# A graph network on one core: sums of messages turned so that their columns lie on partitions

## The chip, the cores and the metric

The kernel runs on one core of a Trainium2 chip. The metric is device time in microseconds (us). Before the change three runs took 4106.76, 4111.01 and 4119.22 us, so the median is 4111.01 us. Lower is better.

The engines are named as in the profile: PE multiplies matrices and PEld is its loading of the side that stays in the array; DVE and ACT work elementwise; POOL here issues the indirect transfers (gathers and scatters); SP issues the plain ones. A product names two operands: the *loaded* side (written into the array first, up to 128 columns) and the *moving* side (streamed through it, up to 512 columns). The result has the loaded side's columns on partitions and the moving side's columns along the free axis. Results go to PSUM.

## The reference

The input is a graph of 6250 nodes with 128 features each and 106250 edges, sorted by destination. Each edge has 64 features and one of 4 types. The first layer is an attention over edges by type, with residual. The second layer, which the change concerns, is:

```
h    = relu(layernorm(x))
e    = concat(h[src_full], h[dst_full], ef_full)      # edges in both directions
msg  = leaky_relu(e @ We1) @ We2                      # 320 -> 256 -> 128
red  = segment_sum(msg, dst_full)                     # per node
x    = x + leaky_relu(concat(h, red) @ Wn1) @ Wn2     # 256 -> 256 -> 128
```

Here `src_full = concat(src, dst)` and `dst_full = concat(dst, src)`, so that each edge sends one message to its destination and one to its source. Since `We2` is linear, the kernel sums the 256 hidden columns per node first and multiplies the sums by `We2` once per node.

## The kernel before

All data are float32. Nodes are packed in 50 blocks (`NU`) of 126: two halves of 63 nodes, each on 64 partitions. Edges of a block are laid in two lots (q = 0, 1) of 9 x 128 places, so that one *step* handles two tiles of 128 edges, and a block takes 9 steps (`TB`); 450 steps in all. After the first layer a table `abtab` holds, per node, both halves of its hidden contribution (2 x 256 columns), and `h2t` holds the transposed node features.

**The loop over edges (lines 1085 to 1137).** For each step: POOL gathers rows of `abtab` by source, two transfers, seven steps ahead (`gather_pair`, issued at line 85). PE forms `z` from edge features and the destination's rows (line 1105). DVE adds the gathered rows (1107), ACT multiplies by 0.01 (1108), DVE takes the maximum (1109): `s` now holds, per edge, 256 columns of the message to the destination and 256 of the message to the source. ACT appends the source's number (1110). POOL scatters the second half to a table `m2d` in memory, two transfers (1113). `s` has four buffers, and a buffer is free again when its scatter has landed and its sums are done.

The message to the destination is summed at once: at lines 1124 to 1126 PE multiplies a one-hot matrix `oh` (128 edges x 64 nodes of a half, the loaded side) with `s` (128 edges x 256 columns, the moving side), into 64 partitions of the PSUM tile `sums`, accumulating over the block's nine steps. Then `add_sums` (979) copies (ACT, 984) or adds (DVE, 982) `sums` into `racc`, an SBUF tile with nodes on partitions and 256 columns for each block.

**The windows (987 to 1018).** The scattered messages, ordered by source in `m2d`, are read back by plain transfers: five parts (`NPT`) of 50 windows, one window per block. A window has 3 to 5 tiles of 128 rows (`window_tiles`): a base of 4, or 3 in the last part, and one more for the blocks near the part's own edges. There are 1012 tiles in all. For each tile DVE makes a one-hot matrix `ohw` (1015), and PE multiplies it (loaded) with the 256 columns of the tile (moving) into `sums2` (1016); the window's sums are added to `racc`. Part j begins in the loop at block `DONE[j]` = 11, 22, 32, 43 and its windows are spread over the steps up to the next one; 11, 10, 11 and 7 blocks. The fifth part follows the loop.

**The last stage (1140 to 1147).** The fifth part's windows run with `node_update` (903) after every four blocks. It transposes `racc` on PE, block by block and half by half (908 to 913: eight transposes and two ACT copies for four blocks), multiplies by `w2` (916), copies to `rdT`, multiplies `hT` and `rdT` by `wn1t` (922, 924), applies the leaky maximum (926), multiplies by `wn2t` (930), adds the residual (938) and writes out (939).

**What sets the order.** The program is written step by step, and a scheduler of the language orders the instructions on each engine by its own estimates of cost; each engine then runs its list strictly in turn. A float32 product is two instructions on PE in this trace: 900 products at line 1105 are 1800 rows.

Of the kernel before, what the change touches and what calls it, by code (L numbers as in the profile page):

```python
# [9 lines left out]
F32 = mybir.dt.float32  # L10
# [4 lines left out]
ALU = mybir.AluOpType  # L15
# [6 lines left out]
P = 128  # L22
# [7 lines left out]
HID = 256  # L30
# [14 lines left out]
NU = -(-N // DB)  # L45
NBK = 2 * NU
NROW = NU * DB + 4
TB = 9
# [41 lines left out]
def kernel(ctx: ExitStack, tc: tile.TileContext, x, src, dst, ef, et, w_rel, a_src, a_dst,  # L90
# [10 lines left out]
    nc = tc.nc  # L101
    ts_, tt, stt, red = (nc.vector.tensor_scalar, nc.vector.tensor_tensor,
                         nc.vector.scalar_tensor_tensor, nc.vector.tensor_reduce)
# [17 lines left out]
    ident = const.tile([P, P], F32, name="ident")  # L121
# [76 lines left out]
    with ExitStack() as prep:  # L198
        cpool = prep.enter_context(tc.tile_pool(name="prep", bufs=1))
        wpool = prep.enter_context(tc.tile_pool(name="prep2", bufs=2))  # L200
        pp = prep.enter_context(tc.tile_pool(name="prepp", bufs=2, space=PSUM))
# [148 lines left out]
        w = CG * TB  # L350
# [541 lines left out]


    c3 = fast.enter_context(tc.tile_pool(name="c3", bufs=1))
    racc = c3.tile([P, NU, HID], F32, name="racc")
    w2 = c3.tile([P, 2, C], F32, name="w2")
    nc.scalar.dma_start(w2, we2.rearrange("(a k) f -> k a f", k=P))
    wn1t = c3.tile([P, 2, HID], F32, name="wn1t")
# [4 lines left out]
    def node_update(wp, pp, b0, nbs):  # L903

        w = nbs * P
        hT = wp.tile([P, 4 * P], F32, name="hT")
        nc.sync.dma_start(hT[:, 0:w], h2t[:, b0 * P:b0 * P + w])
        rT = wp.tile([P, 2, 4 * P], F32, name="rT")
        for a in range(2):
            tp = pp.tile([P, 4 * P], F32, name="tp")  # L910
            for i in range(nbs):
                nc.tensor.transpose(tp[:, i * P:(i + 1) * P], racc[:, b0 + i, a * P:(a + 1) * P], ident)
            nc.scalar.copy(rT[:, a, 0:w], tp[:, 0:w])
        ps = pp.tile([P, 4 * P], F32, name="tp")
        for a in range(2):
            nc.tensor.matmul(ps[:, 0:w], w2[:, a, :], rT[:, a, 0:w], start=(a == 0), stop=(a == 1))
        rdT = wp.tile([P, 4 * P], F32, name="rdT")
        nc.vector.tensor_copy(rdT[:, 0:w], ps[:, 0:w])
        hid = wp.tile([P, 2, 4 * P], F32, name="hid")
        for a in range(2):  # L920
            ph = pp.tile([P, 4 * P], F32, name="ph")
            nc.tensor.matmul(ph[:, 0:w], wn1t[:, 0, a * P:(a + 1) * P], hT[:, 0:w],
                             start=True, stop=False)
            nc.tensor.matmul(ph[:, 0:w], wn1t[:, 1, a * P:(a + 1) * P], rdT[:, 0:w], start=False, stop=True)
            nc.scalar.copy(hid[:, a, 0:w], ph[:, 0:w])
        stt(hid[:, :, 0:w], hid[:, :, 0:w], 0.01, hid[:, :, 0:w], op0=ALU.mult, op1=ALU.max)
        for i in range(nbs):
            po = pp.tile([P, C], F32, name="ph")
            for a in range(2):
                nc.tensor.matmul(po, hid[:, a, i * P:(i + 1) * P], wn2t[:, a, :], start=(a == 0), stop=(a == 1))  # L930
            xr = wp.tile([P, C], F32, name="xr")
            y = wp.tile([P, C], F32, name="y")
            n0 = (b0 + i) * DB
            for q in range(2):
                n1, n2 = n0 + q * GB, min(n0 + q * GB + GB, N)
                h = slice(q * 64, q * 64 + n2 - n1)
                nc.sync.dma_start(xr[h, :], x1r[n1:n2, :])
                tt(y[h, :], po[h, :], xr[h, :], op=ALU.add)  # L938
                nc.sync.dma_start(out[n1:n2, :], y[h, :])
# [5 lines left out]
    with ExitStack() as s4:  # L945
# [33 lines left out]
        def add_sums(b, sums):  # L979

            if b in begun:
                tt(racc[:, b, :], racc[:, b, :], sums, op=ALU.add)
            else:
                nc.scalar.copy(racc[:, b, :], sums)
                begun.add(b)

        def windows(j):

            mts = {}

            def load(b):
                n = window_tiles(j, b)
                mt = mp.tile([P, 5, MW], F32, name="mt")
                r = first_of(st1, j * NU + b, 1, PLACES - n * P)[0]
                ld = nc.sync.dma_start(mt[:, 0:n, :], m2d[ds(r, n * P), :].rearrange("(p i) c -> p i c", i=n))
                if j < NPT - 1:
                    tc.declare_no_dep(ld.ins, group=f"late{j}",
                                      reason="blocks behind a part's last one have no edge of it, or all is done again")
                tc.add_to_no_dep_group("m2", ld.ins)
                mts[b] = mt  # L1000

            for b in range(2):
                load(b)
            yield
            for b in range(NU):
                if b + 2 < NU:
                    load(b + 2)
                n = window_tiles(j, b)
                mt = mts.pop(b)
                at = mp.tile([P, 5], F32, name="at")  # L1010
                ts_(at[:, 0:n], mt[:, 0:n, HID], float(-b * DB), None, op0=ALU.add)
                sums = ps2.tile([P, HID], F32, name="sums2")
                for i in range(n):
                    oh = mp.tile([P, P], F32, name="ohw", bufs=4)
                    ts_(oh, col, at[:, i:i + 1], None, op0=ALU.is_equal)  # L1015
                    nc.tensor.matmul(sums, oh, mt[:, i, 0:HID], start=(i == 0), stop=(i == n - 1))  # L1016
                add_sums(b, sums)
                yield

        with ExitStack() as s5:  # L1020
# [64 lines left out]
            for u in range(NU):  # L1085
                lt, oh = blk.pop(u)
                c0 = 2 * u * TB
                nxt_ = ready(u + 1) if u + 1 < NU else iter(())
                more = u % 5 == 2 and 2 * u + 6 < NBK
                plcs = places(wp, bank, (2 * u + 6) // CG) if more else iter(())  # L1090
                if u in DONE[:-1]:
                    for _ in wins:
                        pass
                    j = DONE.index(u)
                    wins = windows(j)
                    slots = (DONE[j + 1] - u) * TB - 4
                    taken = 0
                sums = pt.tile([P, HID], F32, name="sums")
                for i in range(TB):
                    n = u * TB + i  # L1100
                    if n + AHEAD < NU * TB:
                        gather_pair(n + AHEAD)
                    z = pz.tile([P, 2, 2 * HID], F32, name="z")
                    for q in range(2):
                        nc.tensor.matmul(z[:, q, :], lt[q][:, i * P:(i + 1) * P], rhs[(2 * u + q) % 4], start=True, stop=True)  # L1105
                    s = wp.tile([P, 2, 2 * HID + 1], F32, name="s", bufs=4)
                    tt(s[:, :, 0:2 * HID], z, ags.pop(n), op=ALU.add)  # L1107
                    nc.scalar.mul(z, s[:, :, 0:2 * HID], 0.01)  # L1108
                    tt(s[:, :, 0:2 * HID], s[:, :, 0:2 * HID], z, op=ALU.max)  # L1109
                    nc.scalar.copy(s[:, :, 2 * HID], srcf[:, c0:c0 + 2 * TB].rearrange("p (q i) -> p q i", q=2)[:, :, i])  # L1110
                    for q in range(2):
                        k = c0 + q * TB + i
                        st = nc.gpsimd.indirect_dma_start(  # L1113
                            out=m2d, out_offset=bass.IndirectOffsetOnAxis(ap=placei[:, k:k + 1], axis=0),
                            in_=s[:, q, HID:HID + MW], in_offset=None)
                        tc.declare_no_dep(st.ins, group="m2", reason="each place is written once, and read behind its part")
                        tc.add_to_no_dep_group("m2", st.ins)
                        for j in range(NPT - 1):
                            if u >= DONE[j]:
                                tc.add_to_no_dep_group(f"late{j}", st.ins)  # L1120
                    next(nxt_, None)
                    if i in (1, TB - 1):
                        next(plcs, None)
                    for q in range(2):
                        nc.tensor.matmul(sums[q * 64:(q + 1) * 64, :], oh[:, q * TB + i, :], s[:, q, 0:HID],  # L1125
                                         start=(i == 0), stop=(i == TB - 1))
                    if u >= DONE[0]:

                        t = (u - DONE[sum(u >= d for d in DONE) - 1]) * TB + i
                        while taken * slots <= (t - 2) * (NU + 1):  # L1130
                            next(wins, None)
                            taken += 1
                for _ in nxt_:
                    pass
                add_sums(u, sums)
# [587 lines left out]
```

## Time and profile before

| | before |
|---|---|
| median of three runs | 4111.01 us |
| profiled execution: time, and span within it | 4104.87 us, 4103.1 us |
| mean granted PE clock | 0.878 |
| PE busy | 3053.0 us, 74% of the span |
| POOL busy | 2892.2 us, 70% |
| DVE busy | 2738.6 us, 67% |
| ACT busy | 1545.1 us, 38% |
| edge sums, line 1125, PE | 335.2 us, 1800 instructions |
| window sums, line 1016, PE | 523.3 us, 2024 instructions |
| transposes of `racc`, line 912, PE | 17.6 us, 100 instructions |
| copies of the transposes, line 913, ACT | 13.5 us, 26 instructions |

How to read it: a row of a group gives the line, the engine, the operation, output and inputs, the shapes, how many, and then the busy time in us and the mean duration of one in ns. Durations of PE instructions include the way through the array, so that neighbours overlap; the distance from start to start tells what one costs in a row. A row of the timeline merges neighbours of one kind (`x4`): the start, the time from the first's start to the last's end, and in brackets the idle time of the engine ahead of it with what ended it. "issue" is time in which the engine waited for nothing that the profile shows. The clock that PE was granted stands in the tables by stage (1.00 is full).

### The profile page before, as it was taken

The numbers are of one execution on the slowest core, as the hardware profiler recorded it, in microseconds if no ns is written. First come the engines' busy times: TensorE is split into PE (matmuls) and PEld (weight loads), VectorE is DVE, ScalarE is ACT, GpSimd is POOL, SyncE is SP. The second block draws the span as 40 slices with busy tenths as digits, with TensorE's granted clock in tenths as the row PEclk, the third lists the DMA queues.
The fourth block names the chain that finished last, engine by engine and source line by source line (L and its number), as shares of the span: only waits on it lengthen the run. The fifth ranks groups of instructions, "written<-read, shape, count | busy, mean of one in ns | idle before, by whom it ended". The sixth has DMA issues, their size and how long they took to land. (4 is left out here: it accounts for less than half of the span.)

```text
span 4103.1 us, 43438 instructions
## 1 busy us (share of the span) xinstructions
PE 3053.0 (74%) x11258; PEld 1729.4 (42%) x11258; DVE 2738.6 (67%) x5139; ACT 1545.1 (38%) x2990; POOL 2892.2 (70%) x2887
## 2 busy tenths in 40 slices
PE   4468877778887756666678877778768777688888
PEld 3346555555555532222234342334324333244455
DVE  7467888887777745555466665666657666577755
ACT  3256655566666622222223333222222322222211
POOL 5777787777777527777777777777777777777600
PEclk9669978899999978888899898999989998899999
DMA  7544444455555356666587886888868878588754
GB/s 193 160 101 122 115 114 115 116 123 121 122 129 127 92 135 186 178 178 182 164 252 236 254 249 183 246 245 242 248 198 259 246 234 248 174 260 272 228 167 140
DMA packets 414557, 754.19 MB, mean 184 GB/s; under 512 B 182846, under 2 KB 249380, under 8 KB 414300
## 3 DMA queue, kind: packets, MB, share of 16 engines
q0 software_dynamic: 148800, 430.91, 35.8%
q1 hardware_dynamic: 234314, 290.32, 27.2%
q10 hardware_dynamic: 31186, 30.10, 2.6%
q8 instruction: 92, 1.51, 0.2%
q14 instruction: 165, 1.35, 0.1%
HBM read 586.37 MB, written 164.69 MB: 183 GB/s over the span
## 5 line engine op out<-in xcount | busy, mean ns | idle before, releaser
L85 POOL DMA_INDIRECT xg<-xt,xi x900 | 970.8, 1079 | 274.4 <-issue 224.6
L1113 POOL DMA_INDIRECT m2d<-s,placei x900 | 913.1, 1015 | 294.6 <-issue 211.4
L85 POOL DMA_INDIRECT ag<-abtab,srci x900 | 907.7, 1009 | 294.6 <-issue 205.4
L1105 PE MATMUL z<-rhs,lt 128*128 128x512 f32 x1800 | 1032.5, 701 | 0.6 <-ACT lt L1069 0.6
L1109 DVE TENSOR_TENSOR s<-s,z 128x1024 f32<-128x1024 f32 x450 | 548.1, 1220 | 549.1 <-ACT z L1108 547.7
L1125 PE MATMUL sums<-s,oh 128*64 128x256 f32 x1800 | 335.2, 455 | 491.3 <-DVE s L1109 490.6
L1107 DVE TENSOR_TENSOR s<-z,ag 128x1024 f32<-128x1024 f32 x450 | 549.8, 1222 | 198.8 <-PE z L1105 154.3
L617 PE MATMUL acc<-oh,msg 128*128 128x256 f32 x1800 | 534.3, 435 | 174.2 <-DVE oh L616 168.9
L1108 ACT ACTIVATE z<-s 128x1024 f32<-128x1024 f32 x450 | 461.1, 1025 | 414.8 <-DVE s L1107 413.5
L1105 PEld LDWEIGHTS z<-rhs,lt 128*128 128x128 f32 x1800 | 352.5, 216 | 447.9 <-issue 441.0
L1016 PE MATMUL sums<-mt,ohw 128*128 128x256 f32 x2024 | 523.3, 392 | 8.7 <-DVE ohw L1015 8.7
L1110 ACT COPY s<-srcf 128x2 f32<-128x2 f32 x450 | 86.7, 193 | 1175.8 <-DMA m2d<-s,placei 1159.9
L617 PEld LDWEIGHTS acc<-oh,msg 128*128 128x128 f32 x1800 | 365.2, 216 | 279.7 <-DVE oh L616 210.3
L1016 PEld LDWEIGHTS sums<-mt,ohw 128*128 128x128 f32 x2024 | 389.3, 198 | 198.0 <-issue 128.5
L1125 PEld LDWEIGHTS sums<-s,oh 128*64 128x64 f32 x1800 | 98.6, 149 | 727.6 <-DVE s L1109 579.4
L616 DVE TENSOR_SCALAR oh<-iota,key 128x256 f32<-128x256 f32 x900 | 307.6, 363 | 144.0 <-PE acc L617 136.0
L624 ACT ACTIVATE junk<-dt,nthr 128x1152 bf16<-128x1152 f32 x250 | 312.9, 1252 | 0.2
L1015 DVE TENSOR_SCALAR ohw<-col,at 128x128 f32<-128x128 f32 x1012 | 250.1, 302 | 15.6 <-PE sums L1016 7.9
L1069 ACT COPY lt<-tp 64x384 f32<-64x384 f32 x300 | 141.7, 472 | 108.0 <-PE tp L1065 55.8
L1065 PE MATMUL tp<-ident,fe 128*128 128x128 f32 x450 | 83.6, 292 | 125.5 <-ACT lt L1069 95.6
L607 DVE TENSOR_TENSOR msg<-xg,pw 128x512 f32<-128x512 f32 x225 | 150.8, 684 | 14.6 <-ACT pw L602 14.4
L542 ACT COPY es<-xg 128x128 f32<-128x128 f32 x225 | 62.1, 297 | 221.1 <-DMA xg<-xt,xi 175.8
(417 smaller groups left out, 3227.3 us busy)
## 6 DMA issues: line engine op xcount, KB each, us to landing
mt<-m2d SPq DMA_DIRECT2D x156, 514.0 KB
db<-in_dst_dram SPq DMA_DIRECT2D x200, 288.0 KB
mt<-m2d SPq DMA_DIRECT2D x53, 642.5 KB
dt<-dtyp SPq DMA_DIRECT2D x100, 288.0 KB
fe<-in_edge_attr_dram SPq DMA_DIRECT2D x100, 288.0 KB
mt<-m2d SPq DMA_DIRECT2D x41, 385.5 KB
xg<-xt,xi POOLq DMA_INDIRECT x900
ag<-abtab,srci POOLq DMA_INDIRECT x900
```

The lines of the kernel that those rows point to most:

```text
L85: nc.gpsimd.indirect_dma_start(out=o, out_offset=None, in_=table, in_offset=bass.IndirectOffsetOnAxis(ap=idx.bitcast(I32), axis=0))
L616: ts_(oh.rearrange("p t n -> p (t n)"), iota, key[:, k:k + 1], None, op0=ALU.is_equal)
L617: nc.tensor.matmul(acc[q // 2][:, :, q % 2, :], msg[:, q, :], oh, start=(i == 0 and q % 2 == 0), stop=(i == TB - 1), skip_group_check=True)
L624: nc.scalar.activation(junk, lanes[s]["dt"][v], AF.Sign, bias=nthr[:, u, t:t + 1], accum_out=g[:, v, t:t + 1])
L1015: ts_(oh, col, at[:, i:i + 1], None, op0=ALU.is_equal)
L1016: nc.tensor.matmul(sums, oh, mt[:, i, 0:HID], start=(i == 0), stop=(i == n - 1))
L1105: nc.tensor.matmul(z[:, q, :], lt[q][:, i * P:(i + 1) * P], rhs[(2 * u + q) % 4], start=True, stop=True)
L1107: tt(s[:, :, 0:2 * HID], z, ags.pop(n), op=ALU.add)
L1108: nc.scalar.mul(z, s[:, :, 0:2 * HID], 0.01)
L1109: tt(s[:, :, 0:2 * HID], s[:, :, 0:2 * HID], z, op=ALU.max)
L1113: st = nc.gpsimd.indirect_dma_start(out=m2d, out_offset=bass.IndirectOffsetOnAxis(ap=placei[:, k:k + 1], axis=0), in_=s[:, q, HID:HID + MW ...
L1125: nc.tensor.matmul(sums[q * 64:(q + 1) * 64, :], oh[:, q * TB + i, :], s[:, q, 0:HID], start=(i == 0), stop=(i == TB - 1))
```

## The change

Both kinds of sums swap the sides of their products. The messages become the loaded side, 128 of the 256 columns at a time (a = 0, 1), and the one-hot matrix the moving one. The sums then have a message's columns on partitions and nodes along the free axis. An edge step has four products with 64 moving columns in place of two with 256; a window tile has two with 128 moving columns in place of one with 256. `racc` is kept in that form, two halves of 128 columns for each block, and `node_update` uses it as the moving side of the product with `w2` directly. Its transposes and their copies to `rT` are dropped. Only the first product of a block's sums or of a window carries the start flag.

```diff
-    racc = c3.tile([P, NU, HID], F32, name="racc")
+    racc = c3.tile([P, NU, 2, P], F32, name="racc")
...
-        rT = wp.tile([P, 2, 4 * P], F32, name="rT")
-        for a in range(2):
-            tp = pp.tile([P, 4 * P], F32, name="tp")
-            for i in range(nbs):
-                nc.tensor.transpose(tp[:, i * P:(i + 1) * P], racc[:, b0 + i, a * P:(a + 1) * P], ident)
-            nc.scalar.copy(rT[:, a, 0:w], tp[:, 0:w])
         ps = pp.tile([P, 4 * P], F32, name="tp")
         for a in range(2):
-            nc.tensor.matmul(ps[:, 0:w], w2[:, a, :], rT[:, a, 0:w], start=(a == 0), stop=(a == 1))
+            nc.tensor.matmul(ps[:, 0:w].rearrange("p (n c) -> p n c", n=nbs), w2[:, a, :], racc[:, b0:b0 + nbs, a, :],
+                             start=(a == 0), stop=(a == 1))
...
-                tt(racc[:, b, :], racc[:, b, :], sums, op=ALU.add)
+                tt(racc[:, b], racc[:, b], sums, op=ALU.add)
             else:
-                nc.scalar.copy(racc[:, b, :], sums)
+                nc.scalar.copy(racc[:, b], sums)
...
-                sums = ps2.tile([P, HID], F32, name="sums2")
+                sums = ps2.tile([P, 2, P], F32, name="sums2")
...
-                    nc.tensor.matmul(sums, oh, mt[:, i, 0:HID], start=(i == 0), stop=(i == n - 1))
+                    for a in range(2):
+                        nc.tensor.matmul(sums[:, a, :], mt[:, i, a * P:(a + 1) * P], oh, start=(i == 0 and a == 0),
+                                         stop=(i == n - 1), skip_group_check=True)
...
-                sums = pt.tile([P, HID], F32, name="sums")
+                sums = pt.tile([P, 2, P], F32, name="sums")
...
                     for q in range(2):
-                        nc.tensor.matmul(sums[q * 64:(q + 1) * 64, :], oh[:, q * TB + i, :], s[:, q, 0:HID],
-                                         start=(i == 0), stop=(i == TB - 1))
+                        for a in range(2):
+                            nc.tensor.matmul(sums[:, a, q * 64:(q + 1) * 64], s[:, q, a * P:(a + 1) * P],
+                                             oh[:, q * TB + i, :], start=(i == 0 and q == 0 and a == 0),
+                                             stop=(i == TB - 1), skip_group_check=True)
```

## The prediction

> **What bounds the kernel now.** I read the table of slices first, then the busy time by stage, then the timeline of the engine that is full in each stage, and last the rows of the lines that change. The change touches only the second layer, which starts near 1480 us. Up to there the built order of instructions is the same in both kernels, so the first layer is left alone. Two stages matter: the loop over edges up to about 3900 us, and what follows it. The first two lines here are the loop's last part and its end, the third the stage behind it (columns: stretch; busy us of PE, PEld, DVE, ACT, POOL with counts; granted clock; DMA share; GB/s).
> ```profile
> 3600.00:3866.00 266.00, 227.09 (x829) 126.66 (x828) 196.77 (x394) 73.95 (x131) 204.28 (x203) 0.96 0.88 270
> 3866.00:3908.00 42.00, 28.76 (x108) 14.53 (x106) 27.54 (x48) 9.18 (x15) 19.04 (x20) 0.89 0.38 121
> 3908.00:4096.00 188.00, 179.12 (x774) 121.13 (x774) 113.63 (x385) 28.32 (x52) 0.00 (x0) 0.99 0.54 160
> ```
> In the loop PE has the largest busy time, but it is not the bound. POOL's 203 instructions have 0.30 us of issue ahead of each: 204.28 + 203 x 0.30 = 265.2 of 266 us. The timeline of POOL shows it, four transfers to a step and no other gap:
> ```profile
> 3786.58 1.00 POOL L1113 DMA_INDIRECT m2d<-s,placei  x1 [0.31 <-DVE s L1109]
> 3787.89 0.98 POOL L1113 DMA_INDIRECT m2d<-s,placei  x1 [0.30 <-issue]
> 3789.17 0.99 POOL L85 DMA_INDIRECT ag<-abtab,srci  x1 [0.30 <-DMA ag<-abtab,srci]
> 3790.47 1.01 POOL L85 DMA_INDIRECT ag<-abtab,srci  x1 [0.30 <-DMA m2d<-s,placei]
> 3791.78 1.00 POOL L1113 DMA_INDIRECT m2d<-s,placei  x1 [0.31 <-issue]
> ```
> One step is 3791.78 - 3786.58 = 5.2 us of POOL; the waits of 3600 to 3860 agree. The first line is ACT held until a scatter frees one of the four buffers of `s`: the other engines have run ahead of POOL. The second is PE, in its place in the queue, held for a finished `s`:
> ```profile
> ACT s L1110 <- DMA m2d<-s,placei: 143.0, 44, 8.7
> PE sums L1125 <- DVE s L1109: 31.5, 23, 4.1
> ```
> From 3908 us POOL is idle and PE busy for 179 of 188 us: there PE is the bound, and there a PE instruction saved or added counts in full.
>
> **Edge sums (line 1125), in the loop.** Before, a step issues two products, each as two instructions, with a 64-column load and 256 moving columns. After, it issues four products, eight instructions, each with a 128-column load and 64 moving. Rows for the price, all at full clock:
> ```profile
> 3879.97 0.65 PE L1125 MATMUL sums<-s,oh 128*64 128x256 f32 x4
> 3880.55 1.57 PE L1016 MATMUL sums<-mt,ohw 128*128 128x256 f32 x6
> 1437.05 1.64 PEld L597 LDWEIGHTS pt<-sel,l 128*128 128x128 f32 x14 [1.23 <-ACT l L589]
> 3925.90 1.10 PE L930 MATMUL ph<-wn2t,hid 128*128 128x128 f32 x8
> 3923.74 2.33 PE L1016 MATMUL sums<-mt,ohw 128*128 128x256 f32 x10
> 4001.03 0.60 PE L912 MATMUL tp<-ident,racc 128*128 128x128 f32 x4
> 4001.47 0.60 PE L1016 MATMUL sums<-mt,ohw 128*128 128x256 f32 x2
> ```
> The old four take 3880.55 - 3879.97 = 0.58 us from start to next start. No row has a 128 load with 64 moving, but two stand on either side of it: with 32 moving (line 597) 14 loads take 1.64 us, (1.64 - 0.19)/13 = 0.111 us apart, 0.19 being one load; with 128 moving (line 930) eight take 1.10 us, (1.10 - 0.27)/7 = 0.118 apart, 0.27 being one product. I take 0.115, the middle, and keep 0.111 and 0.13 as ends (0.13 is what line 930 shows in groups of four, 0.52 us each). So 8 x 0.115 = 0.92 us for 0.58: **+0.34 us of PE per step**, over 450 steps 153 us of PE.
>
> What hides it is POOL's 5.2 us. The cover is thinnest in the last part. Where POOL has stopped pacing (3875 to 3889), line 1125 recurs after 4.23, 4.65 and 4.23 us, 4.4 in the mean, with four window tiles in each step: this is what a step costs when PE and its neighbours pace it. Adding 0.34 and four tiles at 0.03 (below) makes 4.86, still under 5.2. Earlier a part has 213 tiles (50 windows of four and 13 of five) to 90 to 99 steps, 2.3 a step, and before 2000 us none, so the cover is thicker. Scatters also wait behind POOL's own queue, and the four-deep ring of `s` takes up single slow steps. I price the loop up to 3866 us at 0; a gain is excluded while POOL sets the pace. If the cover were gone everywhere it would cost those 153 us.
>
> **End of the loop, 3866 to 3908 us.** No gathers are left to issue, so POOL no longer paces. Eight steps' sums remain, five with four tiles: 8 x 0.34 + 20 x 0.03 = 3.3 us if PE holds all of them. Some lines there wait on DVE, which then covers a part (down to 0). I take **+2.5**.
>
> **Window sums (line 1016).** Each tile is one product (two instructions of 256 moving) before and two products (four instructions of 128 moving, 128-column loads) after. Before: ten take 2.33 us, (2.33 - 0.39)/9 = 0.2155 apart, 0.39 being one product; 0.431 a tile. After: 4 x 0.115 = 0.46, **+0.029** (0.111 gives +0.013, 0.13 gives +0.09). Behind 3908 us lie 1012 - 4 x 213 = 160 tiles (the rest are in the loop, hidden with the above): **+4.6**, from +2 to +14.
>
> **Transposes (lines 908 to 913).** 100 transposes go; four take 4001.47 - 4001.03 = 0.44 us, 0.11 each: **-11 us** of PE. The 26 ACT copies of 0.57 us go too, but ACT is busy 28 of 188 us, so this takes only a link out of the chain of a group, where the product at line 916 waited about 0.1 us. It now waits for the last DVE addition into `racc`; the built order puts three window products ahead of it (0.65 us), against one product's end, an addition of 0.42 us and two hand-overs. Products of `wn2t` behind it (line 930) stand eight in a row oftener, with two banks for four outputs, and can wait for DVE's additions. The transposes that filled such gaps are gone as well. A group of four blocks takes 15.07 us (line 912 at 4015.28 and again 15.07 later), and PE's own spacings in it add up to 12.9: 2.1 us idle. A quarter of this either way is +-0.5 x 12.5 groups = +-7 us; nothing tells the sign, so 0.
>
> The additions and copies on `racc` move the same 256 elements per partition (415 and 370 ns now). Queues of SP and POOL get the same issues in the same sequence, so neither carries a term.
>
> **Sum.** 0 + 2.5 + 4.6 - 11 = -3.9 us. The profiled execution took 4104.87 us (span 4103.1 and 1.8 around it): 4101. The three timed runs have a median of 4111.0, 6.1 above it, so I forecast **4107**.
>
> **A rule that speaks against it.** Eight pairs of line 930 stand 0.118 us apart, where the product alone needs 0.108 (half of 0.2155, for half of 256 columns): their 128-column loads lie beside the products. The Trainium skill, "TensorE: Matmul & The Clock Gate", section "Part 3: Packing small matmuls — row/col tiling", says that a load overlaps running products only when its row group differs; here all 128 rows are used by both. By that rule, as an estimate, the load's own 0.108 would be added to every pair, 0.215 with 128 moving and 0.16 with 64, and the sum would be 83 in the loop's last part, 57 behind it and 14 between, about +150 us. The row decides against the rule, and nothing above uses it.
>
> **Rivals.** *Faster:* the idle in the last stage goes with the transposes and the ACT copy, because a group's chain from window sums to output is shorter. For it: ACT's hand-over disappears and PE is the bound. Against: the waits for `rdT` and `hid` stay, with less small work to fill them. Half of the 2.1 us in 12.5 groups is -13, in all -17: 4094 on the median's level. *Slower:* PE takes over from POOL in the last part of the loop. A step there costs 4.4 + (8t - 0.58) + 4(4t - 0.431) = 2.1 + 24t us with t us from pair to pair, and passes 5.2 at t = 0.129. At t = 0.14 it is 5.46: 0.26 x 51 steps (266/5.2) = +13; the last stage 160 x (0.56 - 0.431) - 11 = +10; the end of the loop 8 x 0.54 + 20 x 0.13 = +7; in all +30: 4141. For it: line 930 shows 0.13 in places, some windows have five tiles, and the clock is 0.96, not 1, in that part. Against: the ring of `s` is full there, 143 us of waits. *Not as said:* transposes that come back elsewhere; the built order has none and 1800 + 2024 products for 900 + 1012, so this is left out.
>
> **Chances.** 0.3% of 4111 is 12 us, about what a measurement of this kernel tells from no change. The forecast with its own range, 4097 to 4119: 0.6. Faster rival 0.2, slower rival 0.2. The range runs from 4086 to 4141, with both rivals at their price in it.
>
> **What would show it.** Right: POOL stays at 5.2 us a step; sums of edges take some 0.9 us for eight; the wait of ACT for scatters shrinks; a last-stage group takes 14.2 to 15 us. Wrong: POOL waits for DVE's `s` in steps with windows, pairs are 0.13 us or more apart, or a group takes under 13.8 or over 15.5 us.

## The result, and the profile after

The changed kernel takes 4121.44 us in the median of 12 runs (4110.70 to 4133.09), the kernel before 4110.45 us in the runs beside it (4106.01 to 4119.22): a ratio of 1.0028, 95% interval [1.0018, 1.0038]. That is 11 us more, where the forecast was 4 us less. The profiled run of the changed kernel took 4124.61 us (span 4122.9, granted clock 0.872), 3.2 us above its median; the one before lay 5.6 us below its own. So of the 19.8 us between the two spans some 9 are chance, and stages may be read from the pair only with that in mind.

The experiments come in five groups: beside the first four the kernel before took 4734 to 4797 us, beside the fifth 4111 us (on the chip that had taken 4791 us beside the fourth), so each ratio below is to the kernel before of its own group, and the groups are marked slow or fast machine.

The same stretches as those of the prediction, the first two shifted by the 18 us that the loop ends later, the third by 19 (columns: stretch; busy us of PE, PEld, DVE, ACT, POOL with counts; granted clock; DMA share; GB/s), changed kernel:
```profile
3618.00:3884.00 266.00, 236.49 (x1374) 177.83 (x1374) 195.08 (x389) 72.35 (x130) 203.22 (x199) 0.95 0.87 267
3884.00:3926.00 42.00, 30.75 (x186) 22.80 (x184) 26.74 (x47) 8.99 (x14) 17.47 (x18) 0.91 0.36 108
3927.00:4115.00 188.00, 173.21 (x992) 129.32 (x992) 115.21 (x384) 14.79 (x26) 0.00 (x0) 0.99 0.53 160
```
PE is busy for 9 us more in the loop's last part and for 5.9 us less in the last stage (179.12 before). In the first stretch POOL issues 199 transfers where it issued 203: it no longer keeps its pace everywhere. The groups of the page say the same of the products (line, engine, operation, times it runs, busy us, mean ns, idle before it and what ended most of that):
```profile
L1123 PE MATMUL sums<-oh,s 128*128 128x64 f32 x3600 | 543.6, 301 | 412.6 <-DVE s L1106 411.2
L1012 PE MATMUL sums<-ohw,mt 128*128 128x128 f32 x4048 | 539.6, 283 | 16.8 <-DVE ohw L1010 15.0
L1107 ACT COPY s<-srcf 128x2 f32<-128x2 f32 x450 | 86.5, 192 | 1043.3 <-DMA m2d<-s,placei 1029.6
```
The wait of ACT for scatters fell from 1159.9 to 1029.6 us: ACT stands less often before a ring of `s` that has no free buffer. From the starts of the scatters (line 1110) each stage can be timed; here are the two kernels and, already, the two experiments on the fast machine (us; a step is one of the 450, nine to a block, so steps 9 to 99 are the 90 steps of blocks 1 to 10, which the expectations call blocks 1 to 11; tiles of windows run from step 99 on; POOL's idle is what each gap of over 0.35 us between its transfers has beyond 0.305 us of issue):

| stage | before | after | early old (e8b) | warmed (e10b) |
|---|---|---|---|---|
| steps 9 to 99, no tiles | 475.8 | 486.8 | 480.1 | 482.0 |
| steps 99 to 387 | 1529.9 | 1532.9 | 1535.9 | 1535.4 |
| steps 387 to 441 | 284.4 | 290.7 | 289.6 | 284.9 |
| step 441 to the last scatter | 33.0 | 34.5 | 35.2 | 34.7 |
| last scatter to last product | 193.7 | 193.5 | 194.7 | 192.9 |
| POOL's idle over its issue time, steps 9 to 441 | 17.5 | 32.8 | 29.2 | 26.7 |
| of it in steps 9 to 99 | 5.4 | 14.7 | 7.9 | 11.4 |
| of it in steps 99 to 441 | 12.1 | 18.1 | 21.3 | 15.4 |

The loop, forecast at nothing, has grown; the last stage, forecast 6.4 us shorter, has not moved.

### The profile page after: what moved, and what is told of

Same layout as the page of the kernel before. It is cut to its first block, busy times and chain, and to the rows that moved or that the text cites. A ratio compares the mean times of both kernels' runs of the same rounds, so it can differ in the third digit from the quotient of the medians.

```text
span 4122.9 us, 51024 instructions
## 1 busy us (share of the span) xinstructions
PE 3190.7 (77%) x14982; PEld 2211.3 (54%) x14982; DVE 2749.2 (67%) x5139; ACT 1532.0 (37%) x2964; POOL 2897.2 (70%) x2887
## 4 chain that ended last, share of the span: by engine, by line
PE 28%; DMA 23%; POOL 15%; DVE 13%; issue 12%; ACT 6%; SPq 1%; ACTq 0%; DVEq 0%; POOLq 0%
DMA m2d<-s,placei 12%; PE z L1102 6%; PE acc L617 5%; POOL ag L85 5%; POOL m2d L1110 5%; POOL xg L85 4%; PE sums L1123 4%; PE sums L1012 4%; DMA ag<-abtab,srci 4%; DMA xg<-xt,xi 3%; DVE s L1106 3%; DVE s L1104 3%; DMA mt<-m2d 2%; ACT z L1105 2%; PE lg L538 1%
## 5 line engine op out<-in xcount | busy, mean ns | idle before, releaser
L1102 PE MATMUL z<-rhs,lt 128*128 128x512 f32 x1800 | 1016.6, 692 | 0.6 <-ACT lt L1066 0.6
L1123 PE MATMUL sums<-oh,s 128*128 128x64 f32 x3600 | 543.6, 301 | 412.6 <-DVE s L1106 411.2
L1123 PEld LDWEIGHTS sums<-oh,s 128*128 128x128 f32 x3600 | 509.2, 216 | 561.7 <-DVE s L1106 478.1
L617 PE MATMUL acc<-oh,msg 128*128 128x256 f32 x1800 | 545.1, 442 | 160.7 <-DVE oh L616 154.0
L1012 PEld LDWEIGHTS sums<-ohw,mt 128*128 128x128 f32 x4048 | 528.7, 199 | 167.3 <-issue 133.2
L1012 PE MATMUL sums<-ohw,mt 128*128 128x128 f32 x4048 | 539.6, 283 | 16.8 <-DVE ohw L1010 15.0
L1107 ACT COPY s<-srcf 128x2 f32<-128x2 f32 x450 | 86.5, 192 | 1043.3 <-DMA m2d<-s,placei 1029.6
```

The source lines that it names most:

```text
L617: nc.tensor.matmul(acc[q // 2][:, :, q % 2, :], msg[:, q, :], oh, start=(i == 0 and q % 2 == 0), stop=(i == TB - 1), skip_group_check=True)
L1012: nc.tensor.matmul(sums[:, a, :], mt[:, i, a * P:(a + 1) * P], oh, start=(i == 0 and a == 0), stop=(i == n - 1), skip_group_check=True)
L1123: nc.tensor.matmul(sums[:, a, q * 64:(q + 1) * 64], s[:, q, a * P:(a + 1) * P], oh[:, q * TB + i, :], start=(i == 0 and q == 0 and a == 0) ...
```

## Where the loop's time came from

At full clock the cover was there. In the part with five tiles to a step (timeline, changed kernel):
```profile
3865.16 1.10 PE L1123 MATMUL sums<-oh,s 128*128 128x64 f32 x8 [1.23 <-DVE s L1106]
3866.10 2.45 PE L1012 MATMUL sums<-ohw,mt 128*128 128x128 f32 x20
3868.39 1.88 PE L1102 MATMUL z<-rhs,lt 128*128 128x512 f32 x4
3870.11 1.00 PE L1123 MATMUL sums<-oh,s 128*128 128x64 f32 x8
3870.95 2.45 PE L1012 MATMUL sums<-ohw,mt 128*128 128x128 f32 x20
3873.23 1.88 PE L1102 MATMUL z<-rhs,lt 128*128 128x512 f32 x4
3875.08 1.10 PE L1123 MATMUL sums<-oh,s 128*128 128x64 f32 x8
```
The eight instructions of the edge sums hold PE for 0.84 to 0.94 us until the next line starts (0.92 was forecast), the twenty of the windows take 2.45 us, (2.45 - 0.27)/19 = 0.115 us apart, the price that was taken. A step of five tiles takes 4.95 us here, still under POOL's 5.2.

But not every step is at full clock. Every 40 to 100 us a scatter lands late (in blocks 1 to 10 of the changed kernel ACT waits over 6 us for one at 1635, 1678, 1775, 1817, 1872 and 1971 us; waits of over 5 us there are 7, in the kernel before 8). In the two rows below PE has stood still for 5.47 and 6.38 us, and comes back at half clock. The same place before and after the change, first the kernel before:
```profile
1966.40 0.19 ACT L1110 COPY s<-srcf 128x2 f32<-128x2 f32 x1 [6.59 <-DMA m2d<-s,placei]
...
1968.84 1.12 PE L1125 MATMUL sums<-s,oh 128*64 128x256 f32 x4 [5.47 <-DVE s L1109]
...
1969.89 4.68 PE L1105 MATMUL z<-rhs,lt 128*128 128x512 f32 x6
...
1973.50 0.99 POOL L85 DMA_INDIRECT ag<-abtab,srci  x1 [2.20 <-DVE s L1107]
```
and the changed kernel:
```profile
1971.26 0.19 ACT L1107 COPY s<-srcf 128x2 f32<-128x2 f32 x1 [8.24 <-DMA m2d<-s,placei]
...
1973.69 1.97 PE L1123 MATMUL sums<-oh,s 128*128 128x64 f32 x8 [6.38 <-DVE s L1106]
...
1975.45 5.04 PE L1102 MATMUL z<-rhs,lt 128*128 128x512 f32 x6
...
1979.00 0.99 POOL L85 DMA_INDIRECT ag<-abtab,srci  x1 [2.85 <-DVE s L1104]
```
The six instructions of `z` take 4.68 and 5.04 us there, where four took 1.88 us in the rows above. The edge sums hold PE from 1968.84 to 1969.89, 1.05 us, before, and from 1973.69 to 1975.45, 1.76 us, after: +0.71 where 0.34 was priced. POOL waits 0.65 us longer for DVE's addition, which frees a slot of its gathers, and in the changed kernel it waits for one twice more, 0.75 us at 1982.02 and 0.53 us at 1989.90, where the kernel before has no second wait of over 0.5 us. In such a place PE, not POOL, is the last to be ready, in both kernels, and most of what is added to PE is passed on to POOL.

Late scatters are not the only stalls. Where the last part's windows begin, DVE stands before a late load of a window, with the maximum that finishes `s` behind it in its queue (changed kernel):
```profile
3601.86 0.17 DVE L1006 TENSOR_SCALAR at<-mt 128x4 f32<-128x4 f32 x1 [14.21 <-DMA mt<-m2d]
...
3603.21 1.97 PE L1123 MATMUL sums<-oh,s 128*128 128x64 f32 x8 [13.56 <-DVE s L1106]
...
3603.44 1.00 POOL L1110 DMA_INDIRECT m2d<-s,placei  x1 [3.79 <-DVE s L1106]
```
The kernel before stalls at the same place (DVE 14.50 us, POOL 2.49 us at 3591.69). What ends last there is the load, not PE, so the 1.3 us more of POOL cannot simply be put down to PE's sums. At 3832.67 a wait of PE of 1.77 us, again behind a late load of a window, is followed by half clock from 3833.4 to 3836.8: twenty instructions of the windows take 3.88 us for 2.45, and the step takes 6.58 us. No experiment took these stalls away.

## Experiments

The theory after the result: (H) the loss lies in blocks 1 to 10, where PE is granted half clock for 184 of the 440 us from 1560 to 2000 (167 in the kernel before), so that a step passes POOL's 5.2 us; and (L) the last stage's gain went into late loads. Rivals: PE's added work or its added instructions count anywhere; chance between executions.

**One part alone (slow machine).** Old edge sums in the new layout; old window sums; transposes put back; one more buffer for gathers. All edits are shortened.
```diff
-for a in range(2): matmul(sums[:, a, q*64:(q+1)*64], s[:, q, a*P:(a+1)*P], oh[:, q*TB+i, :])
+matmul(sums[q*64:(q+1)*64, :], oh[:, q*TB+i, :], s[:, q, 0:HID])            # e1
-for a in range(2): matmul(sums[:, a, :], mt[:, i, a*P:(a+1)*P], oh)
+matmul(sums, oh, mt[:, i, 0:HID])                                           # e2
+four transposes of racc and a copy to rT per half, w2's product from rT     # e3
-ag = wp.tile(..., bufs=AHEAD + 2)
+ag = wp.tile(..., bufs=AHEAD + 3)                                           # e4
```


> The changed kernel with the edge sums alone put back to two products of 256 moving columns; window sums and last stage stay as changed. The two kinds of sums then meet in racc in different layouts, so the output is not the reference's; the work and its waits are those of a mixed kernel. Theory A (the loss in the loop comes from the edge sums: eight instructions for four, dear above all at half clock in the first eleven blocks, where no window is summed yet): the stretch from step 9 to step 99, 475.7 us before and 486.8 after, comes back to 476 +-3, step 387 to 441 (284.4 before, 290.7 after) to about 286, and the time to 0.998 to 1.001 of before. Rival B (the window sums with their doubled loads hold up the loop): step 9 to 99 still comes back, for no window is in it, but the time stays at 1.002 to 1.004. Rival C (a chance of the profiled run, or the order that the scheduler made): step 9 to 99 stays near 487.

> The changed kernel with the window sums alone put back to one product of 256 moving columns; edge sums and last stage stay as changed. The layouts in racc are mixed, so the output is not the reference's. Theory A (edge sums cost the loop): step 9 to 99 stays at 487 +-4, time 1.002 to 1.003 of before. Rival B (window sums cost it): time 0.999 to 1.001. On the last stage, 192.6 us from the last scatter's issue being done to the last product, the spacing of the products (30 in 3.53 us, 0.112 apart) gives 160 x (0.45 - 0.43) = 3 us less at most; if loads of windows set that stage, nothing.

> The changed kernel with the eight transposes and two ACT copies for four blocks put back into the node update, though racc is already turned (so the output is not the reference's). My prediction priced them at 11 us of PE on the path. Theory D (the last stage is no longer held by PE but by what feeds it, loads of windows that wait for a free buffer and behind other transfers in SP's queue): the last stage grows from 192.6 us by 0 to 5 us, time 1.003 to 1.004 of before. As predicted (PE holds the stage): it grows by 9 to 12 us, time 1.005 to 1.006.

> The changed kernel with ten buffers in place of nine for the gathered rows; same order of gathers, output as the reference. In the profile of the changed kernel POOL waits 19.9 us between 1560 and 2060 us for DVE's addition to free such a buffer (7.8 before). Theory A1 (PE is late only in bursts at half clock, and the gathers' buffers are the slack that ends first): step 9 to 99 falls from 486.8 to 478-482 us and the time to 1.000 to 1.002 of before. Rival A2 (PE is the bound there for long stretches, so the wait only moves): it stays at 485-488 us and 1.002 to 1.004.

Measured, to the kernel before at 4752 us: new windows alone (e1) 1.011 [1.0075, 1.0145], new edges alone (e2) 1.0076 [1.0048, 1.0104], all with the transposes (e3) 1.0185 [1.0155, 1.0216], all with the buffer (e4) 1.0178 [1.0148, 1.0208]. Both halves cost, and their costs add up. The expectations had a machine at 4111 us in mind; what they would tell apart there is not told apart here. The last stage took 192.3, 195.5, 196.1 and 192.5 us: putting the transposes back (e3) costs 3.6 us there against e4, not 11, and with the old window sums (e2) it was no shorter, though 3 us less were expected at most.

**Clock, early blocks, loads (slow machine).** The changed kernel again (a1); eight idle products in each step of blocks 0 to 10 (e7); old edge sums in these blocks (e8); a fourth buffer of messages loaded three windows ahead and the output written from ACT's queue (e9).
```diff
+if u < DONE[0]:                                                             # e7
+    warm = ps2.tile([P, 2, P], F32, name="sums2")
+    for a in range(8): matmul(warm[:, a % 2, :], ident, ident)
+if u < DONE[0]: matmul(sums[q*64:(q+1)*64, :], oh[:, q*TB+i, :], s[:, q, 0:HID])   # e8
-mt = mp.tile([P, 5, MW], F32, name="mt")                                    # e9
+mt = mp.tile([P, 5, MW], F32, name="mt", bufs=4)
-load(b + 2)
+load(b + 3)
-nc.sync.dma_start(out[n1:n2, :], y[h, :])
+nc.scalar.dma_start(out[n1:n2, :], y[h, :])
```


> The changed kernel once more, unaltered, so that the other three runs of this call stand beside it on the same chip. On a chip like the first: ratio 1.003 to the kernel before, blocks 1 to 11 (90 steps) in some 487 us, last stage some 192.6 us.

> The changed kernel with eight products of ident by ident (128 x 128 columns, about 0.9 us of PE at full clock) behind the edge sums of every step of blocks 0 to 10, into a bank of PSUM that nobody reads. The theory: in these blocks PE is granted half clock for some 180 of 440 us because it has too little to do, and at half clock the changed step's products take longer than POOL's 5.2 us; with more products the granted clock rises to what it is in steps with window tiles (0.95 to 1), a step takes about 4.4 us of PE, and POOL paces. Then the 90 steps of blocks 1 to 11 fall from about 487 us to 470 to 480 us, and the whole is 6 to 15 us faster than the changed kernel. The rival, that PE's amount of work or its number of instructions is what the time of these blocks follows: then 90 steps get longer by up to 90 x 0.9 = 81 us, and the whole is 20 to 80 us slower.

> The changed kernel with the edge sums of blocks 0 to 10 made as before (one-hot matrix loaded, 256 columns of messages moving); it leaves their columns in another layout, so the output is not the reference's and only the time counts. Theory: the 90 steps of blocks 1 to 11 go back from about 487 to about 476 us, everything behind them keeps its time, and the whole is about 11 us faster than the changed kernel, so about level with the kernel before. Rival, that the 11 us of these blocks are chance between executions: the time of the 90 steps stays within 3 us of the changed kernel's in this call.

> The changed kernel with a fourth buffer for a window's messages, its load issued three windows ahead for two, and the writes of the output on ACT's queue, so that loads no longer queue behind a write that waits for y. Theory: in the last stage PE saved its 6.4 us, and lost them again in front of window sums (nine gaps, 5.9 us), because loads arrive late; then the last stage, from the last scatter to the last product, falls from 192.6 to 184 to 188 us. Rival, that the lost time lies with PE's own order of products (wn2t's eight in a row waiting for additions): the last stage stays at 191 to 194 us. The loop may gain 0 to 3 us from earlier loads.

Measured, to 4797 us: a1 1.0181 [1.0146, 1.0215], e7 1.0260 [1.0222, 1.0298], e8 1.0164 [1.0123, 1.0204], e9 1.0157 [1.0123, 1.0191]. The 90 steps took 545.6, 571.2, 538.1 and 539.3 us: a1 and e9, both with the new sums, differ by 6 us, e8 with the old ones and e9 by 1. With the idle products of e7, 42 of 362 instructions of `z` last over 0.75 us (most at full clock last 0.6 us, most at half clock 1.1) for 115 of 359 in a1, and the 90 steps still got 25 us longer: a higher clock did not pay for them. H finds no support here. L finds little: with loads a window earlier PE's waits in front of window sums fell from 12.5 us in 7 to 8.4 us in 2, but 4.7 us in 7 appeared in front of line 919, which waits for `rdT`, and the last stage took 191.3 us for 192.7.

**Instructions or PE time (slow machine).** The kernel before with idle products in all 450 steps: four small ones (d1) or a wide one (d2) of about the same PE time; the kernel before itself (b1); the changed kernel with the wide one in blocks 0 to 10 (e10).
```diff
+dm = ps2.tile([P, 4 * P], F32, name="sums2")
+for k in range(4): matmul(dm[:, k*64:(k+1)*64], ident, ident[:, 0:64])      # d1
+matmul(dm, ident, rhs[(2 * u) % 4])                                         # d2; e10: if u < DONE[0]
```


> The kernel before, unaltered, so that its trace and its stage times are there on the chip of this call. On a chip like the first: 4105 to 4115 us, blocks 1 to 11 in 476 us, the next 288 steps in 1530, the last stage in 193. On a chip like those of the experiments so far (kernel before at 4752 and 4797 us, engines that halt for 1 to 10 us with nothing in the trace that releases them): some 4770 us, and the 288 steps with window tiles in some 1720 us, for 1764 and 1766 with one half of the change and 1810 to 1840 with all of it.

> The kernel before with four idle products in each of the 450 steps (ident loaded, 64 columns of ident moving, into a bank that nobody reads): 3600 more pairs of a load and a product, some 0.92 us of PE a step at full clock. Theory A, that on the slower chips each PE instruction adds time whatever it does (some 0.022 us a pair, from the runs so far): 3600 x 0.022 = +80 us, ratio 1.017 there. Theory B, that added PE time is what counts, since PE paces the steps there: 450 x 0.92 = 414 us of PE, of which the change's rate (about 90 us for some 180 of added PE time, a half) would pass on 100 to 400 us, ratio 1.02 to 1.08. On a chip like the first, where POOL paces at 5.2 us: 5.2 is passed in steps with tiles at half clock only, 0 to +60 us.

> The kernel before with one idle product in each of the 450 steps (ident loaded, 512 columns moving): 900 more pairs, some 0.86 us of PE a step at full clock, so about the same PE time as the run with four small ones and a quarter of the instructions. Theory A (number of instructions): 900 x 0.022 = +20 us, ratio 1.004 on a slower chip. Theory B (PE time): within 10% of what the run with four small ones adds, ratio 1.02 to 1.08. On a chip like the first: the same as the run with many within 10 us.

> The changed kernel with one idle product (ident loaded, 512 columns moving, some 0.86 us of PE at full clock) in every step of blocks 0 to 10 only. Theory of the half clock: on a chip like the first, where PE was granted half clock for 184 of 440 us in these blocks, the clock rises, and the 90 steps of blocks 1 to 11 fall from 487 to 470 to 480 us; if instead PE's work there sets their time at any clock, they get longer by 10 us or more. On the slower chips the run before with eight small idle products took 571 us for 546 without; with one large product theory A expects 546 to 555, theory B 565 to 580.

Measured, to 4734 us: b1 1.0008 [0.9985, 1.0031], d1 1.0390 [1.0322, 1.0459], d2 1.0116 [1.0064, 1.0169], e10 1.0214 [1.0166, 1.0262]. So +188 us for 3600 pairs of load and product (busy 522 us) and +57 us for 900 pairs (498 us): neither theory has its number, but pairs come closer. The two runs differ in more than the number of pairs, though: their pages have 125.8 us of idle PE in front of the idle products of d1 and 29.5 us in d2, most of it with no releaser on the core (93.8 and 12.6 us). In e10 the 90 steps took 541.4 us, less than either theory had. Over the runs on the slow machine a pair added costs 0.02 to 0.06 us (the change adds 1800 + 2024 - 100 = 3724 of them, and 90 us in a1: 0.024), a spread of 3, where a us of PE added at full clock costs 0.15 (d2) to over 2 (e1). Why a pair costs that is open. One candidate was not tested: the queue `q8 instruction` of the pages grows with the pairs (92 packets in the kernel before, 99 in d2, 120 in d1, 122 in a1), though a packet takes as long on either machine (1.0 us). What can be seen is that POOL does not set the pace there. Three rows of the page of the kernel before on the fast machine,
```profile
L1113 POOL DMA_INDIRECT m2d<-s,placei x900 | 913.1, 1015 | 294.6 <-issue 211.4
L85 POOL DMA_INDIRECT ag<-abtab,srci x900 | 907.7, 1009 | 294.6 <-issue 205.4
L1107 DVE TENSOR_TENSOR s<-z,ag 128x1024 f32<-128x1024 f32 x450 | 549.8, 1222 | 198.8 <-PE z L1105 154.3
```
and of the same kernel on the slow one (b1):
```profile
L1113 POOL DMA_INDIRECT m2d<-s,placei x900 | 917.5, 1019 | 444.8 <-issue 243.8
L85 POOL DMA_INDIRECT ag<-abtab,srci x900 | 895.9, 995 | 469.1 <-issue 268.3
L1107 DVE TENSOR_TENSOR s<-z,ag 128x1024 f32<-128x1024 f32 x450 | 549.3, 1223 | 603.8 <-remote 252.8
```
Operations last as long as ever (1.02, 1.00, 1.22 us); what grows is idle time, much of it with no releaser on the core (`remote`). A step with tiles takes 6.0 us for 5.3.

**Rings and DVE's queue (slow machine).** The changed kernel (a2); ten one-hot matrices for four, and the copy `rdT` on ACT for DVE (e12); five buffers of `s` for four and ten one-hot matrices (e13); the same buffers in the kernel before (b2).
```diff
-oh = mp.tile([P, P], F32, name="ohw", bufs=4)
+oh = mp.tile([P, P], F32, name="ohw", bufs=10)                              # e12, e13, b2
-nc.vector.tensor_copy(rdT[:, 0:w], ps[:, 0:w])
+nc.scalar.copy(rdT[:, 0:w], ps[:, 0:w])                                     # e12
-s = wp.tile([P, 2, 2 * HID + 1], F32, name="s", bufs=4)
+s = wp.tile([P, 2, 2 * HID + 1], F32, name="s", bufs=5)                     # e13, b2
```


> The changed kernel unaltered, as the level for the other three on the chip of this call. On a chip like the first: ratio 1.003, 90 steps of blocks 1 to 11 in 487 us, last stage 193.5. On a chip like the three since: ratio 1.018, the 288 steps with window tiles in 1800 to 1830 us for 1739 before, last stage 192 to 193.

> The changed kernel with the copy of w2's product (rdT) on ACT, which idles in the last stage, in place of DVE, and ten buffers for the one-hot matrices of the windows in place of four. Theory: in the last stage DVE's queue stands still while the copy waits for PE (13 us in 11 waits), the one-hot matrices behind it come late, and PE waits for them; with both out of the way the last stage falls from 192 to 193 us to 184 to 188 us on any chip, and the whole by as much (0.1 to 0.2%). Rival, that the chain of a group from its last addition over w2, wn1t, hid and wn2t holds PE whatever DVE does ahead: the last stage stays at 190 to 194 us.

> The changed kernel with five buffers of s in place of four and ten one-hot matrices in place of four. Theory that the rings are too short on the slower chips: the changed kernel gains more from them than the kernel before does, and the two come within 1% of each other (ratio of this to the kernel before with the same buffers 1.00 to 1.01). Rival, that PE's added work and instructions count by themselves: that ratio stays at 1.016 to 1.02, whatever both gain. On a chip like the first, where POOL paces: within 0.2% of the changed kernel.

> The kernel before with the same larger rings: five buffers of s and ten one-hot matrices. On a chip like the first within 0.2% of the kernel before, since POOL paces. On the slower chips both theories leave open what it gains by itself (0 to 2%); what counts is the distance to the changed kernel with the same buffers.

Measured, to 4791 us: a2 1.0206 [1.0130, 1.0281], e12 1.0136 [1.0063, 1.0209], e13 1.0171 [1.0094, 1.0249], b2 0.9985 [0.9955, 1.0015]. The distance between e13 and b2 is 4874.12/4783.38 = 1.019: longer rings do not take it away, and that theory falls. The one on DVE's queue is not borne out: with DVE freed of the copy the last stage took 196.5 us, for 191.9 in a2. It is not ruled out either, because ACT, which now waits for PE with the copy, keeps DVE waiting for `hid`: 22.5 us for 2.6 in a2.

**Early blocks again (fast machine).** The kernels of e8 and e10 once more.

> The changed kernel with the edge sums of blocks 0 to 10 made as before, once more (their columns are left in another layout, so the output is not the reference's). On a chip like the first, theory of the half clock: ratio to the kernel before 0.999 to 1.001 and 474 to 478 us for the 90 steps of blocks 1 to 11; rival (chance): 1.002 to 1.004 as for the changed kernel, and the 90 steps anywhere between 474 and 488. On a slower chip, from what was measured there: 534 to 540 us for the 90 steps with the old sums, 538 to 546 with the new ones, ratio 1.016 to 1.02.

> The changed kernel with one idle product of 512 columns in every step of blocks 0 to 10, once more. On a chip like the first, theory of the half clock: the 90 steps take 470 to 480 us, and fewer than 60 of the products of z in them are at half clock (86 of 271 were); rival: 487 us or more. On a slower chip: 541 us again, within the 538 to 546 of the changed kernel, though only 48 of 265 products of z ran at half clock for 79 of 268; ratio 1.018 to 1.024.

Measured, to 4111.35 us: e8b 1.0026 [1.0015, 1.0037], e10b 1.0018 [1.0006, 1.0029]. H, as it was stated, falls: with the old sums in blocks 0 to 10 the whole should have come back to 0.999 to 1.001, and 9.5 of the 11 us remain. POOL's waits from 1560 to 2060 us in the kernel before, the changed kernel and e8b, in this order (us in total, times, longest):
```profile
POOL ag L85 <- DVE s L1107: 7.8, 9, 2.2
POOL ag L85 <- DVE s L1104: 19.9, 21, 2.9
POOL ag L85 <- DVE s L1104: 9.1, 8, 2.2
```
So some 11 us of one profile hang on these sums, about what the 90 steps grew by (486.8 for 475.8). The times do not confirm it: e8b is 9.5 us over its kernel before, the changed kernel was 11.0 over its own, a difference of 1.5 us, give or take 6. e10b came out between its expectations in these steps (482.0 us; 470 to 480, or 487 and more). One place shows what warming could not do. Its timeline, behind a late scatter:
```profile
1784.12 1.97 PE L1123 MATMUL sums<-oh,s 128*128 128x64 f32 x8 [6.91 <-DVE s L1106]
...
1785.88 4.65 PE L1102 MATMUL z<-rhs,lt 128*128 128x512 f32 x6
...
1789.44 0.99 POOL L85 DMA_INDIRECT ag<-abtab,srci  x1 [2.85 <-DVE s L1104]
```
The idle product stands in PE's queue behind the sums that wait, so it can't run while PE stands still: the sums after the stall take 1.97 us as before, although over the 90 steps only 65 of 360 instructions of `z` last over 0.75 us, for 118 of 362 in the changed kernel. (The expectation counted distances between neighbours, 58 of 270 for 86 of 271; some of those have edge sums between them.)

## Why the prediction was wrong, point by point

- **Loop priced at 0: the step that failed.** The prediction compared means, 4.86 us of PE at full clock against 5.2 of POOL, let the ring of `s` take up single slow steps, and took the blocks without tiles for the safest. The means hold (4.95 us with five tiles). What does not hold is that slow steps are taken up: steps 9 to 441 took 2302.3 to 2310.4 us in the three traces with the change for 2290.0, and POOL's idle in them rose by 9 to 15 us (26.7, 29.2, 32.8 for 17.5). In blocks 1 to 10 the way can be followed: behind a late scatter PE is at half clock, the edge sums cost 0.71 us more there, not 0.34, and POOL waits 0.65 us longer and once or twice again. That this is most of the loss the times do not bear out: e8b, with the old sums there, keeps 9.5 of the 11 us, give or take 6. From step 99 on the loop took 6.0 to 11.2 us longer (1820.3, 1825.5 and 1823.6 for 1814.3), and POOL's idle there rose by 3 to 9 us. What holds these steps was not tried by an experiment on the fast machine and stays open; late scatters, late loads of windows and PE at half clock behind them are seen, in the kernel before as well. With one trace of the kernel before, itself 5.6 us under its median, part of each figure is chance: the 90 early steps of e8b, with old sums, also took 4.3 us more.
- **End of the loop, +2.5:** 33.0 to 34.5, 35.2 and 34.7, so +1.5 to +2.2. About right.
- **Price of a pair, 0.115 us:** right (0.115 for windows, 0.84 to 0.94 us for eight of edges at full clock). The sentence of the Trainium skill that was weighed ("TensorE: Matmul & The Clock Gate", "Part 3: Packing small matmuls — row/col tiling") would have had, as an estimate, 0.215 for a pair of 128 moving columns; the trace goes against it (0.115), as it did before. The same section excepts a load into the background weight buffer, which the prediction left out.
- **Window tiles +4.6, transposes -11, bubbles 0 +-7 in the last stage:** the sum in PE time is right (PE busy for 5.9 us less), its effect is not. Idle time of PE took its place: of 188 us PE is idle for 14.8 where it was idle for 8.9, and most of what grew stands in front of window sums, before and after:
```profile
L1016 PE MATMUL sums<-mt,ohw 128*128 128x256 f32 x318 | 80.6, 387 | 8.7 <-DVE ohw L1015 8.7
L1012 PE MATMUL sums<-ohw,mt 128*128 128x128 f32 x636 | 82.6, 282 | 15.1 <-DVE ohw L1010 13.4 <-issue 1.3 <-PE ph L925 0.3
```
  The stage took 193.5 to 195.6 us in five traces with the old form, 191.7 to 194.7 in ten with the new: means 194.2 and 192.8, -1.4 for -6.4; on the fast machine alone 193.7 and 193.7. So the bubbles, put at 0, are the mis-sized term, +5 to +6 of the 7 that were allowed. Neither earlier loads (e9) nor a DVE without the copy (e12) gave the time back; the waits moved. What holds the stage instead stays open; a group's chain through w2, wn1t, `hid` and wn2t is left as a candidate, untested.
- **Rivals.** The faster one found nothing. The slower one was right that PE takes over from POOL, but in single steps, not by a pair at 0.129 us or more, nor in the last part alone. The worst case, the cover gone everywhere, was given as 153 us: on the slow machine, where POOL's idle over steps 9 to 441 is 341 us before (b1) and 456 after (a2), the change cost 90 and 96 us (a1, a2).
- Forecast and result lie 15 us apart, -4 and +11. Within what the traces allow, 5 to 6 of them are what the last stage didn't give, and the rest is the loop. No kernel run here beat the kernel before by more than the interval (b2, 0.9985 [0.9955, 1.0015]).

## What to carry to other kernels

An engine that is covered in the mean need not be covered in the steps after a stall: look up the longest waits of the engine that sets the pace, and price the added work there, at the clock that the trace shows right after the stall. PE time saved in a stage can come back as PE's idle time (here 5.9 us of each); and work that is cut into more and smaller products can cost more on a machine in a worse condition than on the one where it was tuned (0.3% and 1.8 to 2.1% for the same change).

## What was not expected of the hardware

- The same chip ran the same kernel in 4791 and, later, in 4111 us. Operations kept their lengths; engines halted, mostly for 1 to 11 us, with no releaser on the core (239 waits of over 1 us in b1, none on the fast machine), and the granted clock was 0.82 for 0.87 to 0.88.
- On the slow machine 3600 small pairs of load and product cost +188 us, 900 wide ones of about the same PE time +57; the idle time in front of them differed as well.
- PE's half clock after 5 to 7 us of standing still lasted over the next eight sums and most of six instructions of `z`, some 5 us, and a wait of 1.77 us could be followed by 3.4 us of it. Some three in ten instructions of `z` in blocks 1 to 10 last over 0.75 us, whichever form the sums had (106 of 359 before, 118 of 362 after, 106 of 360 in e8b).
